# Adding the second Toeplitz combination to Q inside its PSUM bank, with ScalarE as the reader, in a fused conv-attention-STU kernel

## The chip, the cores and the metric

The kernel runs on one core of a Trainium2 chip. The metric is the device time of one execution in microseconds (us), median of three runs. Fractions of a microsecond are given in us unless marked ns. The engines are named PE (TensorE, matrix multiply; PEld is its weight load), DVE (VectorE), ACT (ScalarE), POOL (GpSimd) and SP (the engine that issues the transfers here). SBUF is the on-chip working memory, PSUM the small memory of eight banks that PE writes its results to.

## The reference, cut to what matters

Four batch items of 48 x 48 tokens with 128 channels go through two layers. Layer 0 is a gated selective scan over four directions. Layer 1 is full attention over the 2304 tokens of an item, followed by a spectral filter layer (STU), to which the change belongs:

```python
U_plus, U_minus = _stu_conv(phi, u, PADDED_SL)      # causal convolution of u with 16 filters
s = sigma ** SIGMA_POW
out = jnp.einsum('btkd,k,kde->bte', U_plus, s, Mpp)
out = out + jnp.einsum('btkd,k,kde->bte', U_minus, s, Mpm)
...
out = out + jnp.einsum('btd,de->bte', ui, Mu[i])    # autoregressive part, 3 taps
...
outs over frac in (1, 2, 4, 8): the same on x[:, :T // frac] with other M; summed with weights
```

The kernel does the causal convolutions as products with Toeplitz matrices on PE. It splits tokens by their index modulo 4, so that a convolution over 2304 tokens becomes short ones over 576, and uses the three-product form of a two-by-two convolution: one product with the sum of two inputs (Q), and two others that are each added to Q.

## The kernel before, in words

**Stages.** For each batch item b, `scans(b, ...)` runs layer 0's selective scan; then an epilogue and `attention` follow. PE has little to do in the scans, so other work is laid between their steps by `more(share)`, which draws pieces from a generator until a share of the columns is done. In `scans(0)` that work is `mixture` (weights of the STU); in `scans(1)` to `scans(3)` it is the STU of the item before, `stu_alone(b - 1, ps)`. The STU of the last item runs by itself at the end. So there are three mixed stages and one end stage with an STU.

**A scan unit** (`scan`, lines 453 to 459) is four steps: ACT makes `dA` with an Exp into one of two PSUM banks (`psa`), and DVE scans it (L458). `enter` (L450) and `times_c` (L467) are DVE or POOL products over 1536 columns; `spread` (L442) and `sum_c` (L475) are PE matmuls.

**An STU** goes over `items`: five blocks of rows of `BLOCKS` (0-128, 128-256, 256-384, 384-512, 512-576), 16 filters k each, 80 items. They are called blocks 0 to 4 below. An item makes six convolutions `conv(n, c, g)`: combination c = 0, 1, 2 and group g = 0, 1, in the order (0,0) (0,1) (1,0) (1,1) (2,0) (2,1). Each is a chain of matmuls over row blocks J (L969) into a PSUM tile of the pool `psc`, which has three banks with one tag, used in turn (four in the end stage). What reads the bank is `taken`: for c = 0, ACT copies it into the SBUF tile Q (L983); for c = 1 and 2, DVE writes the sum of the bank and Q into U (L994). This reader is kept in `late` and put into its engine's queue by `do_late`, at the end of the following convolution. `project` (L1031) multiplies the U of the item before with the weights G; it stands after (1,0), the third convolution. At the first item of a block, `end` transposes the last block's result through another `psc` tile, and `ended` (DVE) reads that.

**The Toeplitz tiles.** The moving operands are tiles `tt` (pool of four buffers), loaded by SP from DRAM `fd` (L942), each row overlapping. A tile holds `SLOT` = 1154 columns: all three c in block 0, c = 0 and 1 together and then c = 2 in block 1, one c each in blocks 2 to 4. `fetch(n, c)` is called after each convolution. It looks up the tile that holds c (`held`) and issues loads up to the third tile beyond it. A load waits until PE has read the last of the tile whose buffer it takes, four tiles earlier; it stands in SP's queue with the scans' loads `rep` and `bc`, in order.

All queues are in program order as written out by these generators.

Of the kernel before, what the change touches and what calls it, by code (L numbers as in the profile page):

```python
# [8 lines left out]
F32 = mybir.dt.float32  # L9
# [6 lines left out]
P = 128  # L16
# [38 lines left out]
def hybrid_kernel(ctx: ExitStack, tc: tile.TileContext, a: dict, out: bass.AP):  # L55
# [3 lines left out]
    nc = tc.nc  # L59
# [742 lines left out]
    def mixture(pool, ps):  # L802

        late = []

        def keep_(G, p, j, k, q):
            nc.scalar.copy(G[:, :, j], p)
            if j == 0:  # L810
                nc.sync.dma_start(gd[k, :, q], G.rearrange("p s j c -> p (s j) c"))

        for k in range(KF):
            M = [pool.two.tile([P, NF, C], F32, tag=f"M{j}", name=f"M{j}_{k}") for j in range(2)]
            for t, src in zip(M, ("M_phi_plus", "M_phi_minus")):
                nc.sync.dma_start(t, a[src][:, k].rearrange("i d e -> d i e"))

            W = pool.two.tile([P, 2, NF, P], F32, tag="W", name=f"W{k}")
            for i in range(NF):
                nc.scalar.activation(W[:, 0, i], ident, AF.Copy, scale=ws[:, k, i:i + 1])  # L820
                nc.scalar.activation(W[:, 1, i], nident, AF.Copy, scale=ws[:, k, i:i + 1])
            yield 0
            for q in range(2):
                G = pool.two.tile([P, 3, 2, C], F32, tag="Gm", name=f"Gm{k}_{q}")
                for j in (1, 0):
                    p = ps.psc.tile([P, 3, C], F32, tag="c", name=f"G{k}_{q}_{j}")
                    for i in range(NF):

                        n = NF - 1 - i if j else 1
                        if i == (NF - 1 if j else 0):  # L830
                            continue
                        for t in range(2):
                            nc.tensor.matmul(p[:, :n] if j else p[:, NF - 1 - i], W[:, q if t else 0, i],
                                             M[t][:, i].unsqueeze(1).to_broadcast([P, n, C]) if j else M[t][:, i],
                                             start=(t == 0 and (i == 0 or not j)),
                                             stop=(t == 1 and (i == NF - 2 or not j)))
                            yield n * C
                    if late:
                        keep_(*late.pop())
                    late.append((G, p, j, k, q))  # L840
        keep_(*late.pop())
# [58 lines left out]
    def stu(b, pool, ps):  # L900
# [10 lines left out]

        u, sums = us[b]
        items = [(blk, k) for blk in BLOCKS for k in range(KF)]
        tts, Gs, Q, U, now, nxt = {}, {}, {}, {}, {}, [0]
        late = []

        def do_late(n=0):
            while len(late) > n:  # L920
# [7 lines left out]

        order = [(n, cs) for n in range(len(items)) for cs in slots(n)]

        def fetch(n, c):


            held = next(i for i, (j, cs) in enumerate(order) if j == n and c in cs)
            while nxt[0] < min(held + 4, len(order)):
                i, cs = order[nxt[0]]
                (lo, hi, place, extra), k = items[i]
                w = hi + 1
                t = pool.four.tile([P, SLOT], F32, tag="tt", name=f"tt{b}_{i}_{cs[0]}")
                t = t[:, :2 * len(cs) * w].rearrange("p (e i) -> p e i", i=w)  # L940
                row = fd[k, cs[0], 0]
                nc.sync.dma_start(t, bass.AP(row.tensor, row.offset + LF - hi,  # L942
                                             [[1, P], [LF + P, 2 * len(cs)], [1, w]]))
                for x in cs:
                    tts[i, x] = t[:, 2 * (x - cs[0]):2 * (x - cs[0]) + 2]
                nxt[0] += 1

        def fetch_G(n):
            if n < len(items):
                (lo, hi, place, extra), k = items[n]  # L950
                m = 2 if extra else 1
                Gs[n] = pool.two.tile([P, 2, 2, C], F32, tag="G", name=f"G{b}_{n}")
                nc.sync.dma_start(Gs[n][:, :, :m], gd[k, :, :, place:place + m])

        def conv(n, c, g):

            (lo, hi, place, extra), k = items[n]
            w = hi - lo
            first = lo - (g == 1 and c != 1)
            nw = hi - first  # L960
            t = tts[n, c]
            p = ps.psc.tile([P, 512], F32, tag="c", name=f"cv{b}_{n}_{c}_{g}")
            p2 = p[:, :2 * nw].rearrange("p (e m) -> p e m", e=2)
            nb = (hi + P - 1) // P
            for J in range(nb):
                at = max(first, J * P) if J else first
                end = J * P - 1
                x = (sums[:, J, g], u[:, J, 2 + g], u[:, J, g])[c]
                nc.tensor.matmul(p2[:, :, at - first:], x, t[:, :, hi - 1 - at + J * P:end if end >= 0 else None:-1],  # L969
                                 start=(J == 0), stop=(J == nb - 1))  # L970
                if J < nb - 1:
                    yield 2 * (hi - at)
            do_late()
            late.append(lambda: taken(n, c, g, p, w, nw))
            yield 2 * (hi - at)

        def taken(n, c, g, p, w, nw):
            if c == 0:
                if g == 0:
                    U[n] = pool.two.tile([P, 8 * P], F32, tag="U", name=f"U{b}_{n}")[:, :8 * w].rearrange(  # L980
                        "p (i m) -> p i m", i=8)
                Q[g] = pool.two.tile([P, 2 * (P + 1)], F32, tag=f"Q{g}", name=f"Q{b}_{n}_{g}")[:, :2 * nw]
                nc.scalar.copy(Q[g], p[:, :2 * nw])  # L983
                return

            if g == 0:
                dst, src, q = U[n][:, c - 1::6], p[:, :2 * w], Q[g]
            elif c == 1:
                dst, src = U[n][:, 2:6:3], p[:, :2 * w]
                q = Q[g].rearrange("p (e m) -> p e m", e=2)[:, :, 1:]  # L990
            else:
                dst, src, q = U[n][:, 3:5], p[:, 1:1 + 2 * w], Q[g][:, 1:1 + 2 * w]
            src, q = [x if len(x.shape) == 3 else x.rearrange("p (e m) -> p e m", e=2) for x in (src, q)]
            nc.vector.tensor_tensor(dst, src, q, ALU.add)  # L994

        def begin(n):
# [28 lines left out]
        def project(n):  # L1025
            (lo, hi, place, extra), k = items[n]
            w = hi - lo
            p = now["p"].rearrange("p f r m -> p (f r) m")
            for q in range(2):
                for v, x in reversed(parts(w, extra)):  # L1030
                    nc.tensor.matmul(p[:, :, :v], Gs[n][:, q, x, :], U[n][:, 4 * q:4 * q + 4, :v], start=False,  # L1031
                                     stop=(k == KF - 1 and q == 1 and v == w))
                yield 4 * (w + extra)
            if k == KF - 1:
                late.append(lambda: kept(n, now["p"], w))
# [5 lines left out]
        def end(n):  # L1041
            (lo, hi, place, extra), k = items[n]
            w = hi - lo
            p = ps.psc.tile([P, 4, C], F32, tag="c", name=f"ot{b}_{n}")
            for f in range(2):
                for r in range(2):
                    i = 2 * f + r
                    nc.tensor.transpose(p[:w, 2 * r + f], now["o"][:, i * w:(i + 1) * w], ident)
            late.append(lambda: ended(n, p, lo, hi))
            yield 4 * w  # L1050
# [3 lines left out]
            nc.vector.tensor_tensor(t, t, p[:hi - lo], ALU.add)  # L1054
            nc.sync.dma_start(out[b, 4 * lo:4 * hi].rearrange("(p j) c -> p j c", j=4), t)

        fetch(0, 0)
        for n, (_, k) in enumerate(items):
            if k == 0:
                begin(n)  # L1060
            for c in range(3):
                for g in range(2):
                    yield from conv(n, c, g)
                    fetch(n, c)
                    if (c, g) == (0, 0):
                        fetch_G(n)
                    elif (c, g) == (1, 0) and n > 0:
                        yield from project(n - 1)
                    elif (c, g) == (2, 1) and k == 0:
                        if n > 0:  # L1070
                            yield from end(n - 1)
                        yield from ar(n)
        do_late()
        yield from project(len(items) - 1)
        do_late()
# [44 lines left out]
    start_y(0)  # L1120
    for b in range(B):
        sp = Stage(tc, f"h{b}", "left", s=(6, SB))
        ps = Stage(tc, f"b{b}", "right", psa=(2, PSUM), psy=(1, PSUM), psB=(1, PSUM), psc=(3, PSUM), psp=(1, PSUM))
        bank["mm"] = ps.psB, "B"
        if b == 0:
            mixed = Stage(tc, "m", "right", two=(2, SB))
# [42 lines left out]
        assert first or not more  # L1169
        ps.close()  # L1170
        back.close()
    ps = Stage(tc, "end", "right", psc=(4, PSUM), psp=(1, PSUM))
    for _ in stu_alone(B - 1, ps):
        pass
    ps.close()
# [54 lines left out]
```

## Time and profile before

| | |
|---|---|
| median of 3 runs | 6416.79 us (6412.86 to 6426.66) |
| the profiled execution, and its span | 6422.87 us, 6421.2 us |
| PE busy | 5440.6 us (85%) |
| DVE busy | 4823.6 us (75%) |
| POOL busy | 3842.7 us (60%) |
| ACT busy | 2800.0 us (44%) |
| DMA queue of SP (q1) | 1025.00 MB, 62.3% of 16 engines' span |
| first mixed stage (STU of item 0 beside the scans of item 1) | 1474 to 2597 us |
| end stage (STU of item 3 alone) | 5715 to 6421 us |

Busy shares over the whole span mix stages with different limits, so the prediction reads them by stage. A line of the page's list of groups gives line, engine, operation, tiles written and read, shapes and count; then busy time in us, mean duration in ns, and idle time of the engine just before, with what ended most of it. "A <- B" in a list of waits means that A's engine stood idle until B.

### The profile page before, as it was taken

To read this page: it belongs to the slowest core of one execution; us is meant where nothing else is said; L and a number is where in the kernel's file an instruction comes from. 1 tells how busy PE (TensorE), PEld (TensorE's weight loads), DVE (VectorE), ACT (ScalarE), POOL (GpSimd) and SP (SyncE) were. 2 spreads that over 40 slices of the span, in tenths; PEclk is the share of its full clock that TensorE was granted. 3 is DMA by queue.
4 is the path that set the end of the run, shared out by engine and by line. 5 is a ranking of instruction groups with operands and counts; after the bars stand their busy time and mean duration, and the time that the engine had idled before them with its cause. 6 is when DMAs were issued, how large, how long until landed. Compare 5 with 4: busy or idle time off the path is not lost.

```text
span 6421.2 us, 75575 instructions
## 1 busy us (share of the span) xinstructions
PE 5440.6 (85%) x25032; PEld 3353.1 (52%) x25032; DVE 4823.6 (75%) x6193; ACT 2800.0 (44%) x5053; POOL 3842.7 (60%) x1825
## 2 busy tenths in 40 slices
PE   3656555697999998888999999788999999789999
PEld 1222222444556566544556567544555567547789
DVE  6999999548999998558999998458999999322111
ACT  2555555244555554244555554244555554221000
POOL 1989888406778887306788887207788888100000
PEclk6787777799999999899999999899999999899999
DMA  4556566126878889127878889127788888025546
GB/s 104 139 138 151 139 144 148 40 55 162 199 196 215 216 221 247 59 62 165 198 195 217 222 218 256 39 64 179 189 203 215 219 224 246 28 67 151 154 141 212
DMA packets 658246, 1033.52 MB, mean 161 GB/s; under 512 B 93856, under 2 KB 515872, under 8 KB 633120
## 3 DMA queue, kind: packets, MB, share of 16 engines
q1 hardware_dynamic: 652032, 1025.00, 62.3%
q10 hardware_dynamic: 5824, 3.69, 0.3%
q8 instruction: 200, 3.28, 0.2%
q14 instruction: 190, 1.56, 0.1%
HBM read 905.79 MB, written 122.56 MB: 160 GB/s over the span
## 4 chain that ended last, share of the span: by engine, by line
PE 45%; DVE 24%; DMA 16%; POOL 4%; issue 4%; ACT 4%; SPq 3%; DVEq 0%; ACTq 0%; POOLq 0%
PE cv L969 19%; DVE s L458 11%; PE pr L1031 6%; DVE s L450 5%; DMA tt<-fd 5%; DMA rep<-dtdud 4%; PE s L714 4%; PE y L475 3%; PE o L707 3%; DMA bc<-xdd 3%; POOL s L467 3%; PE op L650 2%; PE B L442 2%; DVE xc L264 2%; DVE re L408 2%
## 5 line engine op out<-in xcount | busy, mean ns | idle before, releaser
L467 POOL TENSOR_TENSOR s<-s,bc 128x1536 f32<-128x1536 f32 x768 | 2647.8, 3449 | 179.8 <-DVE s L458 88.9
L458 DVE TENSOR_TENSOR_SCAN s<-dA,carry,s 128x384 f32<-128x384 f32 x2560 | 2458.1, 1000 | 190.1 <-ACT dA L455 189.0
L455 ACT ACTIVATE dA<-rep,A 128x384 f32<-128x384 f32 x3072 | 1782.0, 585 | 1627.0 <-DVE s L458 1622.2
L969 PE MATMUL cv<-tt,u 128*128 128x256 f32 (+3 forms) x7680 | 1632.6, 351 | 64.3 <-DVE U L994 38.0
L969 PEld LDWEIGHTS cv<-tt,u 128*128 128x128 f32 x7680 | 1259.7, 190 | 583.1 <-issue 266.1
L450 POOL TENSOR_TENSOR s<-rep,bc 128x1536 f32<-128x1536 f32 x288 | 994.2, 3452 | 95.3 <-DMA bc<-xdd 95.3
L969 PE MATMUL cv<-tt,us 128*128 128x256 f32 (+3 forms) x3840 | 841.0, 358 | 106.6 <-DVE U L994 55.3
L994 DVE TENSOR_TENSOR U<-cv,Q 128x256 f32<-128x256 f32 (+1 forms) x1280 | 480.3, 381 | 596.0 <-PE cv L969 581.2
L450 DVE TENSOR_TENSOR s<-rep,B 128x1536 f32<-128x1536 f32 x480 | 832.2, 1734 | 56.1 <-PE B L442 32.8
L475 PE MATMUL y<-s,csum 128*32 128x384 f32 x6144 | 720.6, 544 | 142.4 <-DVE ya L481 85.0
L969 PEld LDWEIGHTS cv<-tt,us 128*128 128x128 f32 x3840 | 639.7, 195 | 323.8 <-DVE U L994 89.7
L1031 PE MATMUL pr<-U,G 128*128 128x512 f32 (+4 forms) x2048 | 694.7, 469 | 3.5 <-DVE U L994 3.2
L983 ACT COPY Q<-cv 128x256 f32<-128x256 f32 (+3 forms) x640 | 224.0, 351 | 1027.2 <-PE cv L969 1025.5
L442 PE MATMUL B<-xd,spread 128*128 128x384 f32 x960 | 443.0, 546 | 177.4 <-DVE s L450 166.8
L458 DVE TENSOR_TENSOR_SCAN s<-dA,s 128x384 f32<-128x384 f32 x512 | 459.3, 938 | 70.9 <-ACT dA L455 70.7
L466 POOL COPY carry<-s 128x4 f32<-128x4 f32 x640 | 121.6, 190 | 574.8 <-DVE s L458 534.5
L1031 PEld LDWEIGHTS pr<-U,G 128*128 128x128 f32 x2048 | 334.5, 190 | 198.2 <-issue 137.0
L714 PE MATMUL s<-xnT 128*128 128x512 f32 (+1 forms) x720 | 357.9, 582 | 42.7 <-ACT xnT L676 23.4
L475 PEld LDWEIGHTS y<-s,csum 128*32 128x32 f32 x6144 | 127.7, 112 | 497.4 <-issue 336.3
L158 POOL TENSOR_TENSOR ln_vu<-ln_vu,mhalf 128x4 f32<-128x4 f32 (+1 forms) x20 | 26.8, 1341 | 602.0 <-DVE ln_vu L157 602.0
L716 ACT ACTIVATE e<-s,shift 128x512 f32<-128x512 f32 (+1 forms) x360 | 231.2, 644 | 314.1 <-PE s L714 313.6
L707 PE MATMUL o<-e,xn 128*128 128x512 f32 (+1 forms) x720 | 343.4, 560 | 4.5 <-ACT e L716 4.5
(157 smaller groups left out, 3638.1 us busy)
## 6 DMA issues: line engine op xcount, KB each, us to landing
rep<-dtdud SPq DMA_DIRECT2D x768, 384.0 KB, 7.8
tt<-fd SPq DMA_DIRECT2D x192, 577.0 KB, 5.5
bc<-xdd SPq DMA_DIRECT2D x2304, 48.0 KB, 3.4
tt<-fd SPq DMA_DIRECT2D x192, 513.0 KB, 4.5
tt<-fd SPq DMA_DIRECT2D x192, 385.0 KB, 4.3
dtdud<-re SPq DMA_DIRECT2D x768, 96.0 KB, 2.3
G<-gd SPq DMA_DIRECT2D x192, 256.0 KB, 5.3
tt<-fd SPq DMA_DIRECT2D x64, 514.0 KB, 5.6
```

Source lines behind the costliest of these rows:

```text
L442: nc.tensor.matmul(self.bt[:, :CS], spread[:, self.ch.k // 2, self.q].rearrange("p c j -> p (c j)"), self.ch.xd, start=True, stop=True)
L450: eng.tensor_tensor(s, self.ch.rep[self.h][:, 1], bt.unsqueeze(1).to_broadcast([P, G4, CS]), ALU.mult)
L455: nc.scalar.activation(dA[:, :CS], ch.rep[self.h][:, 0, g], AF.Exp, scale=A[:, ch.k, self.h * G4 + g, self.q:self.q + 1])
L458: nc.vector.tensor_tensor_scan(s, dA[:, CS - 1::-1] if ch.rev else dA[:, :CS], s, 0.0 if ch.first else carry[:, self.h, self.q, g:g + 1], ...
L467: nc.gpsimd.tensor_tensor(self.s, self.s, ch.bc[Q4 + self.q].unsqueeze(1).to_broadcast([P, G4, CS]), ALU.mult)
L475: nc.tensor.matmul(ch.y[g * DL:(g + 1) * DL, :CS], csum, self.s[:, g], start=(self.q == 0), stop=(self.q == Q4 - 1))
L707: nc.tensor.matmul(po[J][:, :w], xn[:, i], e[:, :w], start=(i == 0), stop=(i == NT - 1))
L714: nc.tensor.matmul(p[:, :w], xnT[:, i * P:(i + 1) * P], xnT[:, 512 * J:512 * J + w], start=True, stop=True)
L716: nc.scalar.activation(e[:, :w], p[:, :w], AF.Exp, bias=shift)
L969: nc.tensor.matmul(p2[:, :, at - first:], x, t[:, :, hi - 1 - at + J * P:end if end >= 0 else None:-1], start=(J == 0), stop=(J == nb - 1))
L994: nc.vector.tensor_tensor(dst, src, q, ALU.add)
L1031: nc.tensor.matmul(p[:, :, :v], Gs[n][:, q, x, :], U[n][:, 4 * q:4 * q + 4, :v], start=False, stop=(k == KF - 1 and q == 1 and v == w))
```

## The change

For c = 2 the matmuls no longer open a new accumulation in a bank of their own: they go on adding into the bank that still holds the c = 0 product of the same group (it has been copied to Q for c = 1). The sum is then already in PSUM, and ACT copies it into U; DVE's sum for c = 2 is gone. DVE still sums for c = 1. The three banks get tags of their own: `q0` and `q1` for the groups' c = 0 and 2, `c` for c = 1 (and for `end`'s transposes). The order of the six convolutions becomes (0,0) (1,0) (0,1) (2,0) (1,1) (2,1), and `fetch` takes the list of convolutions left in the item instead of c: a tile counts as held as long as one of these needs it. `project` of the item before stays after the third convolution, now (0,1). In the end stage each tag has two banks, six in all instead of four. `mixture` goes round the three tags.

```diff
@@ mixture
-                    p = ps.psc.tile([P, 3, C], F32, tag="c", name=f"G{k}_{q}_{j}")
+                    p = ps.psc.tile([P, 3, C], F32, tag=("c", "q0", "q1")[banks[0] % 3], name=f"G{k}_{q}_{j}")
+                    banks[0] += 1
@@ stu
+        banks = {}
+
+        convs = [(0, 0), (1, 0), (0, 1), (2, 0), (1, 1), (2, 1)]
...
-        def fetch(n, c):
-            held = next(i for i, (j, cs) in enumerate(order) if j == n and c in cs)
+        def fetch(n, left):
+            held = next(i for i, (j, cs) in enumerate(order) if j == n and any(c in cs for c, g in left))
...
-            p = ps.psc.tile([P, 512], F32, tag="c", name=f"cv{b}_{n}_{c}_{g}")
+            if c < 2:
+                p = banks[c, g] = ps.psc.tile([P, 512], F32, tag="c" if c else f"q{g}", name=f"cv{b}_{n}_{c}_{g}")
+            else:
+                p = banks[0, g]
...
-                                 start=(J == 0), stop=(J == nb - 1))
+                                 start=(c < 2 and J == 0), stop=(J == nb - 1), skip_group_check=(c == 2))
...
-                dst, src, q = U[n][:, 3:5], p[:, 1:1 + 2 * w], Q[g][:, 1:1 + 2 * w]
-            src, q = [x if len(x.shape) == 3 else x.rearrange("p (e m) -> p e m", e=2) for x in (src, q)]
+                dst, src = U[n][:, 3:5], p[:, 1:1 + 2 * w]
+            src = src.rearrange("p (e m) -> p e m", e=2)
+            if c == 2:
+                nc.scalar.copy(dst, src)
+                return
+            q = q if len(q.shape) == 3 else q.rearrange("p (e m) -> p e m", e=2)
             nc.vector.tensor_tensor(dst, src, q, ALU.add)
...
-            for c in range(3):
-                for g in range(2):
-                    yield from conv(n, c, g)
-                    fetch(n, c)
...
+            for i, (c, g) in enumerate(convs):
+                yield from conv(n, c, g)
+                fetch(n, convs[i:])
+                if i == 0:
+                    fetch_G(n)
+                elif i == 2 and n > 0:
+                    yield from project(n - 1)
+                elif i == 5 and k == 0:
+                    if n > 0:
+                        yield from end(n - 1)
+                    yield from ar(n)
@@ stages
-        ps = Stage(tc, f"b{b}", "right", psa=(2, PSUM), psy=(1, PSUM), psB=(1, PSUM), psc=(3, PSUM), psp=(1, PSUM))
+        ps = Stage(tc, f"b{b}", "right", psa=(2, PSUM), psy=(1, PSUM), psB=(1, PSUM), psc=(1, PSUM), psp=(1, PSUM))
-    ps = Stage(tc, "end", "right", psc=(4, PSUM), psp=(1, PSUM))
+    ps = Stage(tc, "end", "right", psc=(2, PSUM), psp=(1, PSUM))
```

More of the change, by code (lines that the diff above doesn't have):

```diff
@@ L806, in mixture @@
         late = []
+        banks = [0]
         def keep_(G, p, j, k, q):
@@ L1055, in ended @@
             nc.sync.dma_start(out[b, 4 * lo:4 * hi].rearrange("(p j) c -> p j c", j=4), t)
-        fetch(0, 0)
+        fetch(0, convs)
         for n, (_, k) in enumerate(items):
@@ L1060, in stu @@
                 begin(n)
-            for c in range(3):
-                for g in range(2):
-                    yield from conv(n, c, g)
-                    fetch(n, c)
[L1065 to L1072, printed above, removed]
+            for i, (c, g) in enumerate(convs):
[9 more added lines that the diff above has]
+                    yield from ar(n)
         do_late()
```

## The prediction

> **What bounds the kernel now.** I read the page's slices first, to see which stages the change touches.
>
> ```profile
> PE   3656555697999998888999999788999999789999
> ...
> DVE  6999999548999998558999998458999999322111
> ...
> DMA  4556566126878889127878889127788888025546
> ```
>
> Each digit is 160 us. The Toeplitz work (L969) lies in the three stretches where PE, DVE and DMA all stand at 8 or 9 (the mixed stages), and in the last five slices (the end stage), where DVE is nearly idle. The groups give the change's prices: sum, copy, and the scan that DVE is there for.
>
> ```profile
> L458 DVE TENSOR_TENSOR_SCAN s<-dA,carry,s 128x384 f32<-128x384 f32 x2560 | 2458.1, 1000 | 190.1 <-ACT dA L455 189.0
> ...
> L994 DVE TENSOR_TENSOR U<-cv,Q 128x256 f32<-128x256 f32 (+1 forms) x1280 | 480.3, 381 | 596.0 <-PE cv L969 581.2
> ...
> L983 ACT COPY Q<-cv 128x256 f32<-128x256 f32 (+3 forms) x640 | 224.0, 351 | 1027.2 <-PE cv L969 1025.5
> ```
>
> Then busy time in windows, cut at the blocks of the first mixed stage (block 0 to 4 downward; columns: window, length, busy PE, PEld, DVE, ACT, POOL with counts, clock, DMA share, GB/s).
>
> ```profile
> 1474.00:1630.00 156.00, 136.44 (x554) 72.51 (x554) 137.61 (x184) 78.81 (x148) 114.15 (x57) 0.97 0.76 179
> 1630.00:1839.00 209.00, 194.97 (x880) 113.35 (x880) 191.08 (x241) 107.36 (x195) 166.97 (x74) 0.96 0.78 190
> 1839.00:2094.00 255.00, 245.07 (x1179) 150.08 (x1178) 247.55 (x297) 140.18 (x246) 217.33 (x99) 0.99 0.88 217
> 2094.00:2392.00 298.00, 285.10 (x1371) 179.67 (x1370) 291.77 (x344) 161.59 (x282) 264.28 (x121) 0.99 0.85 219
> 2392.00:2597.00 205.00, 182.46 (x1339) 144.73 (x1339) 177.50 (x229) 93.12 (x175) 159.15 (x73) 0.95 0.87 232
> ```
>
> In blocks 2 and 3 DVE is 97-98% busy and PE 96%: two engines are at their limit together. In block 4 both drop to under 90% while the transfers are densest. The waits of that whole stage (1474 to 2597 us) say what stands between them:
>
> ```profile
> ACT Q L983 <- PE cv L969: 135.6, 92, 9.5
> ...
> DVE s L458 <- ACT dA L455: 69.2, 59, 5.3
> ...
> PE cv L969 <- DVE U L994: 31.4, 27, 3.9
> PE cv L969 <- DMA tt<-fd: 17.2, 5, 5.1
> ```
>
> Last, the timeline of PE, ACT and DVE at 2438 us, in block 4:
>
> ```profile
> 2437.98 2.91 PE L969 MATMUL cv<-tt,us 128*128 128x128 f32 x12 [5.13 <-DMA tt<-fd]
> ...
> 2440.49 0.27 ACT L983 COPY Q<-cv 128x128 f32<-128x128 f32 x1 [5.95 <-PE cv L969]
> ...
> 2441.28 1.02 DVE L458 TENSOR_TENSOR_SCAN s<-dA,carry,s 128x384 f32<-128x384 f32 x1 [5.34 <-ACT dA L455]
> ```
>
> A late tile stops PE for 5.13 us; ACT stands at the copy behind it for 5.95 us, with the next Exp in its queue, and DVE starves for 5.34 us. So in block 4 a late tile reaches the scans in full.
>
> **What the Trainium skill says.** "TensorE: Matmul & The Clock Gate", section on the architectural detail of the array, calls the ACT and DVE queues strict FIFO; the three lines above agree. "PSUM — Partial Sum Buffer", section "The four PSUM rules", allows a synchronised read of a partial sum in the middle of an accumulation group; the new c = 2 rests on that, and no run here shows it yet.
>
> **The change part by part.** Mixed stages count three times, the end stage once.
>
> *DVE sums removed.* Per stage 160 of 320 sums go: 128 of 256 columns (median 0.398 us) and 32 of 128 columns (0.267 us), so 50.9 + 8.5 = 59.5 us of DVE, 51 us of it in blocks 0 to 3. That is no path time: PE is idle only 56 us in these four blocks together (918 us less 861.6 busy), and with DVE eased PE is the limit. What I credit is PE's own wait for these sums: 31.4 us per stage, halved because half the banks are now read by ACT: 16 us, 48 us in all. Bounds: 0 and 51 us per stage. In block 4 and in the end stage DVE is no limit: nothing.
>
> *Copies added on ACT.* 160 per stage, taken as the Q copy's 0.351 us: 56 us, ACT from 581 to 637 us of 1123. In blocks 2 and 3 the scan is longer than the Exp (1000 against 585 ns), which hides a copy. In blocks 0 and 1 ACT already waits 83 us (1475 to 1950 us) for PE at its Q copies, and behind a waiting copy stands an Exp. The trace has no such copy for c = 2; bounds are 0 and another 69 us per stage (today's whole starvation). I take 4 us: 12 us in all.
>
> *PE.* The same matmuls; each bank is reused three convolutions after it was written, as before. The copy of Q must be done before (2,g) writes; two convolutions lie between, and PE waited for Q copies only 3.5 us per stage. Nothing.
>
> *`end`.* Its transposes now take bank `c`, whose sum (1,1) is queued on DVE one convolution before instead of two, and (1,0) of the next item then waits for `ended`. Four times per stage; the one such wait that shows is 3.1 us (ot <- U). Lower bound 0, upper 4 x 2 x 3 = 24 us; much of it lies under DVE's backlog: 3 us per stage, 9 us in all. The end stage has two such banks: nothing.
>
> *Toeplitz tiles.* This is the part that decides. With one c per tile (blocks 2 to 4), a tile was read by two neighbouring convolutions; now c = 0 spans positions 0-2, c = 1 positions 1-4, c = 2 positions 3-5. With four buffers, tile (n+1, c = 1) takes the buffer of (n, c = 0): from its last read to its first use lay six convolutions, and now lie four. The same for c = 2; c = 0 keeps six. Bytes, loads and SP's order are the same. I matched in the trace, for each load of the three stages, the last matmul on the old buffer, issue, landing and first use (medians, first mixed stage, us):
>
> | tile | lead before | release to issue | issue to landing | lead after |
> |---|---|---|---|---|
> | block 2, c=1 | 15.5 | 1.4 | 6.9 | 10.9 |
> | block 3, c=1 | 18.4 | 2.2 | 5.1 | 12.9 |
> | block 4, c=1 | 13.1 | 1.9 | 5.9 | 7.9 |
> | block 4, c=2 | 12.4 | 0.0 | 6.3 | 8.7 |
> | end stage, block 4, c=1 | 7.4 | 0.0 | 4.5 | 5.2 |
>
> Landing times spread (block 4 of the stage):
>
> ```profile
> DMA to landing us min/median/max: 3.6/6.3/12.6
> ```
>
> Shifting each load by the new release and use, c = 1 in block 4 is late in 9 or 10 of 16 items, by 26, 29 and 28 us in the three stages together; c = 2 by 6 to 9 us; blocks 2 and 3 together by 14, 9 and 22 us. The end stage misses by 0.1 us: nothing. These sums are no forecast yet: a stall at c = 1 gives c = 2 its time back, and fewer loads under way land sooner (4.5 us in the end stage). I take 15 of block 4's 28 us, and 5 of the 15 us of blocks 2 and 3, where DVE has a backlog under which PE may wait: 20 us per stage, 60 us in all. Bounds: 5 us per stage if landings fall to the end stage's, and about 50 us if all of it stays (152 us in three stages).
>
> **Sum:** -48 + 12 + 9 + 60 = +33 us. The profiled execution's own time is 6422.87 us (span 6421.2 and 1.7 around it) and would be 6456; it lies 6.1 us over the median, so against the median 6416.79 this is 6450 us.
>
> **The rivals.**
>
> *Likeliest, chance 0.43: shallower prefetch outweighs the relief,* 6430 to 6490.
>
> *Relief wins, 0.26, faster.* Place: blocks 0 to 3 of the mixed stages. If DVE is the true limit, 35 of its 51 us come back: -105 us, against 12 + 9 + a prefetch loss of 8 per stage (24): -60, so 6357 us. It decides from the point where relief per stage exceeds late tiles per stage plus 7 us. For it: DVE 97-98% busy for 553 us. Against: PE is at 96% in the same windows, and 59.5 us is the most that goes.
>
> *ACT becomes the gate, 0.19, slower still.* The tiles cost 30 us per stage, and ACT's doubled copies, each waiting for PE, starve the scans by 20 more: -48 + 90 + 60 + 9 = +111, so 6528 us. For it: the 2438 us chain. Against: in blocks 2 and 3 (1950 to 2420 us) ACT waits at Q copies only 11 us.
>
> *No difference, 0.12:* relief and late tiles cancel, or the reordering adds waits that hold the old pace.
>
> **How the numbers follow.** About 0.2% (13 us) is what a measurement can tell from no change. Slower 0.43 + 0.19 = 0.62, same 0.12, faster 0.26. Predicted 6450. The likeliest case alone spans 6430 to 6490. The range leaves out half of the faster case's lower tail and the upper tail of the ACT case: 6355 to 6530.
>
> **What would show it.** Right: 640 DVE sums instead of 1280, and 640 copies into U on ACT at 0.27 to 0.37 us; PE waiting for `tt` well over 17.2 us per mixed stage, mostly in block 4; block 4 longer than its 205 us by some 15 us; blocks 0 to 3 (918 us) shorter by about 10 us; the end stage within 2 us of its 706 us. Wrong: block 4 not longer (then landings have eased), blocks 0 to 3 shorter by over 25 us per stage (then DVE was the limit, not PE), or the scan's wait for Exp well over 69 us per stage outside block 4 (then ACT is the gate).

## The result, and the profile after

The changed kernel took 6405.99 us (median of 4 runs, 6404.10 to 6408.92) against 6414.82 us for the kernel before; ratio 0.9985, 95% interval 0.9968 to 1.0003. Measured again with 14 runs against 18: 6402.16 against 6413.73 us, **ratio 0.9981 (0.9973 to 0.9989)**. So the change makes the kernel 12 us faster, a little under the 0.2% that the prediction set as its bound, where 33 us slower was predicted.

The page of the changed kernel: the slices, and the groups that answer to those shown of before.

```profile
PE   3665565697999998888999998788999998889999
...
DVE  6999999548889998458899998458899998311000
...
DMA  4556566127888888127888888127888887025546
...
L458 DVE TENSOR_TENSOR_SCAN s<-dA,carry,s 128x384 f32<-128x384 f32 x2560 | 2442.5, 1000 | 246.3 <-ACT dA L455 244.1
...
L1007 DVE TENSOR_TENSOR U<-cv,Q 128x256 f32<-128x256 f32 (+1 forms) x640 | 244.4, 382 | 688.3 <-PE cv L978 679.9
...
L1004 ACT COPY U<-cv 128x256 f32<-128x256 f32 (+1 forms) x640 | 222.9, 348 | 676.1 <-PE cv L978 675.2
...
L992 ACT COPY Q<-cv 128x256 f32<-128x256 f32 (+3 forms) x640 | 223.0, 348 | 378.7 <-PE cv L978 375.2
```

The sums are halved and 640 copies into U stand on ACT, at 348 ns, as expected. DVE's busy time fell from 4823.6 to 4622.7 us, that is by 201 us, and the time by 12. The first mixed stage in windows, cut at its blocks (columns as in the prediction):

```profile
1471.00:1619.00 148.00, 131.83 (x554) 72.92 (x554) 125.28 (x151) 87.24 (x177) 110.99 (x56) 0.99 0.79 186
1619.00:1826.00 207.00, 193.59 (x881) 113.36 (x882) 185.28 (x213) 117.67 (x230) 167.75 (x74) 0.98 0.80 194
1826.00:2084.00 258.00, 246.27 (x1178) 151.69 (x1177) 236.71 (x264) 148.88 (x277) 219.48 (x100) 0.98 0.87 214
2084.00:2381.00 297.00, 286.74 (x1376) 181.07 (x1375) 281.67 (x314) 170.27 (x315) 264.60 (x122) 0.99 0.86 221
2381.00:2587.00 206.00, 183.29 (x1337) 144.97 (x1335) 170.89 (x195) 97.56 (x206) 158.47 (x72) 0.94 0.82 229
```

In blocks 2 and 3 DVE went from 97-98% to 92-95% busy; PE stands at 95-97% as before. The waits of that stage (1471 to 2587 us):

```profile
ACT U L1004 <- PE cv L978: 108.3, 86, 8.1
DVE s L458 <- ACT dA L455: 89.3, 78, 7.7
ACT Q L992 <- PE cv L978: 47.2, 34, 9.5
PE cv L978 <- DMA tt<-fd: 27.8, 15, 5.1
...
PE cv L978 <- DVE U L1007: 19.5, 17, 3.9
```

Beside before: PE waits 12 us less for DVE's sums (19.5 for 31.4), 11 us more for tiles (27.8 for 17.2), and the scan 20 us more for its Exp (89.3 for 69.2). A chain like the one at 2438 us before is still there, in block 4 at 2526 us (timelines of PE, ACT, DVE):

```profile
2526.40 4.14 PE L978 MATMUL cv<-tt,u 128*128 128x128 f32 x22 [5.07 <-DMA tt<-fd]
...
2528.91 0.27 ACT L1004 COPY U<-cv 128x128 f32<-128x128 f32 x1 [8.10 <-PE cv L978]
...
2529.69 1.93 DVE L458 TENSOR_TENSOR_SCAN s<-dA,carry,s 128x384 f32<-128x384 f32 x2 [7.68 <-ACT dA L455]
```

Now the copy for c = 2 is what holds the Exp back. The time by block, from the first Toeplitz matmul of a block to the first of the next one (block 4 and the end stage: to the last matmul), worked out from the traces, three mixed stages added up (us):

| kernel | block 0 | block 1 | block 2 | block 3 | block 4 | end stage |
|---|---|---|---|---|---|---|
| before | 468.6 | 632.8 | 763.2 | 895.9 | 599.3 | 699.0 |
| after | 442.3 | 617.7 | 769.9 | 888.2 | 622.7 | 700.7 |
| difference | -26.3 | -15.1 | +6.7 | -7.7 | +23.4 | +1.7 |

A gain in blocks 0, 1 and 3 and a loss in block 4 nearly cancel. PE's wait for tiles rose by 37 us in the three stages, half of it in block 4 and half in blocks 2 and 3, where it was nothing before.

### The profile page after: what moved, and what is told of

Read it like the earlier page. It is cut to its first block, busy times and chain, and to the rows that moved or that the text cites. A ratio compares the mean times of both kernels' runs of the same rounds, so it can differ in the third digit from the quotient of the medians.

```text
span 6402.6 us, 75570 instructions
## 1 busy us (share of the span) xinstructions
PE 5427.8 (85%) x25032; PEld 3364.4 (53%) x25032; DVE 4622.7 (72%) x5553; ACT 2980.6 (47%) x5693; POOL 3840.5 (60%) x1825
## 4 chain that ended last, share of the span: by engine, by line
PE 49%; DVE 20%; DMA 17%; POOL 4%; issue 4%; ACT 4%; SPq 3%; DVEq 0%; ACTq 0%; POOLq 0%
PE cv L978 22%; DVE s L458 8%; PE pr L1044 7%; DMA tt<-fd 6%; DMA rep<-dtdud 4%; PE y L475 4%; DVE s L450 4%; PE s L714 4%; DMA bc<-xdd 3%; PE o L707 3%; POOL s L467 3%; PE B L442 2%; PE op L650 2%; DVE xc L264 2%; DMA G<-gd 2%
## 5 line engine op out<-in xcount | busy, mean ns | idle before, releaser
L467 POOL TENSOR_TENSOR s<-s,bc 128x1536 f32<-128x1536 f32 x768 | 2646.4, 3447 | 177.3 <-DVE s L458 93.3
L978 PE MATMUL cv<-tt,u 128*128 128x256 f32 (+3 forms) x7680 | 1649.9, 354 | 131.2 <-DMA tt<-fd 68.1
L978 PE MATMUL cv<-tt,us 128*128 128x256 f32 (+3 forms) x3840 | 855.4, 352 | 35.2 <-DMA tt<-fd 26.0
L1007 DVE TENSOR_TENSOR U<-cv,Q 128x256 f32<-128x256 f32 (+1 forms) x640 | 244.4, 382 | 688.3 <-PE cv L978 679.9
L1004 ACT COPY U<-cv 128x256 f32<-128x256 f32 (+1 forms) x640 | 222.9, 348 | 676.1 <-PE cv L978 675.2
L714 PE MATMUL s<-xnT 128*128 128x512 f32 (+1 forms) x720 | 356.9, 581 | 44.7 <-ACT xnT L676 23.4
```

Source lines behind the costliest of these rows:

```text
L467: nc.gpsimd.tensor_tensor(self.s, self.s, ch.bc[Q4 + self.q].unsqueeze(1).to_broadcast([P, G4, CS]), ALU.mult)
L714: nc.tensor.matmul(p[:, :w], xnT[:, i * P:(i + 1) * P], xnT[:, 512 * J:512 * J + w], start=True, stop=True)
```

## The experiments

All times are medians; ratios are to the kernel before on the same chip, with 95% intervals. Three chips were used, with the kernel before at 6413.73 us (the first four kernels), 6415.01 us (`order5`, `after5`, `dve_twice`, `hyb03`) and 6413.90 us (`before5`, `hyb5`, `order5_p3`), so the chips differ by about 1 us. The interval of a single ratio is wider: about 8 us each way for most kernels here, 5 us for `after_2` and `before5`.

**The changed kernel again** (`after_2`).

> The changed kernel once more, for a tighter interval. Blocks 0 to 3 of the three mixed stages together were 42 us shorter in the first profile and block 4 of them 23 us longer, the end stage 2 us longer. If that balance holds, the ratio lies at 0.997 to 0.999 with an interval that now excludes 1; if the first result was chance, the ratio is within 0.0005 of 1.

6402.16 us, 0.9981 (0.9973 to 0.9989): the small gain is real.

**The new order alone** (`order_only`): PSUM and readers as before.

```diff
-            if c < 2:
-                p = banks[c, g] = ps.psc.tile([P, 512], F32, tag="c" if c else f"q{g}", name=f"cv{b}_{n}_{c}_{g}")
-            else:
-                p = banks[0, g]
+            p = ps.psc.tile([P, 512], F32, tag=("c", "q0", "q1")[banks[0] % 3], name=f"cv{b}_{n}_{c}_{g}")
+            banks[0] += 1
...
-            if c == 2:
-                nc.scalar.copy(dst, src)
-                return
```

> The kernel before with the new order of convolutions and the new fetch alone: c = 2 again has a bank of its own in the rotation of three, and VectorE sums it with Q. Theory 1 (two effects: VectorE's relief gives some 14 us per mixed stage, the shallower prefetch of Toeplitz tiles takes some 9): no relief, the prefetch loss stays, so 20 to 40 us slower than before, ratio 1.003 to 1.006, with PE waiting for tiles 22 to 29 us per mixed stage and block 4 longer by 3 to 12 us per stage. Rival 3 (the order itself is what brings the gain, by spreading the readers of the banks): 5 to 20 us faster than before, with blocks 0 and 1 shorter by about 10 us per stage.

6482.01 us, 1.0102 (1.0089 to 1.0116): 68 us slower than before, so the order is no source of the gain (rival 3 falls), and it costs far more than theory 1 said. PE's wait for tiles is 24 to 28 us per mixed stage, within the expectation; block 4 grew by 21 us over three stages, but blocks 0 to 2 by 6, 7 and 26 us, where PE's wait for tiles rose by under 5 us in all. What the change does beyond the order is worth 80 us (6402 against 6482).

**DVE instead of ACT reads the bank** (`dve_reader`): accumulation and order stay.

```diff
-                nc.scalar.copy(dst, src)
+                nc.vector.tensor_copy(dst, src)
```

> The changed kernel with VectorE instead of ScalarE copying the c = 2 sum out of its bank: the accumulation in PSUM and the order stay, the reader does not move. Theory 1: VectorE saves only the second operand, so its relief is nearly nothing while the prefetch loss stays: 25 to 45 us slower than the changed kernel, ratio to before 1.003 to 1.006. Rival 2: PE waits for VectorE at the banks as before (31 us instead of 19 us per mixed stage), 20 to 40 us slower than the changed kernel too; the two part at the kernel with VectorE's time put back. If ScalarE's copies are a burden on the scan's Exp (rival ACT), this kernel is as fast as the changed one or faster, and the scan waits for Exp less than before (52 to 57 us per stage outside block 4 would fall to 40 or less).

6465.87 us, 1.0082 (1.0069 to 1.0096): 64 us slower than the changed kernel, more than either theory said. Its group of copies on the page, and waits of its first mixed stage (1470 to 2602 us):

```profile
L1004 DVE COPY U<-cv 128x256 f32<-128x256 f32 (+1 forms) x640 | 244.8, 383 | 395.8 <-PE cv L978 394.1
...
DVE s L458 <- ACT dA L455: 47.9, 43, 4.5
PE cv L978 <- DVE U L1004: 27.2, 22, 3.9
PE cv L978 <- DVE U L1007: 11.5, 14, 1.7
```

At 383 ns the copy costs DVE what the sum did (381 ns): accumulating in PSUM saves none of DVE's time as long as DVE reads the bank. Of the 80 us, some 16 belong to the accumulation, for a reason that no run shows, and 64 to the move to ACT. PE's wait for DVE at the banks is 39 us (27.2 and 11.5), against 19.5 in the changed kernel; the second and third stage differ by as much, so the move takes about 60 us of these waits away (5 come back as waits for ACT's copies). The scan's wait for Exp is 48 us, against 89 in the changed kernel; `dve_twice` below says how much of that goes with ACT's copies.

**DVE's time put back, first try** (`dve_load`).

```diff
                 nc.scalar.copy(dst, src)
+                idle = pool.one.tile([P, 2 * (P + 1)], F32, tag="idle", name=f"idle{b}_{n}_{g}")
+                nc.vector.tensor_tensor(idle[:, :2 * w], Q[g][:, :2 * w], Q[g][:, :2 * w], ALU.add)
                 return
```

> The changed kernel with VectorE's time put back: beside each ScalarE copy of c = 2 VectorE adds Q to itself into an unused tile (two SBUF inputs, the same columns as the sum that went). Nothing waits for its result. Theory 1 (VectorE's time is what was relieved): the 42 us of blocks 0 to 3 are gone, so 30 to 50 us slower than the changed kernel, ratio to before 1.004 to 1.007. Rival 2 (VectorE's time is worth nothing, PE is the limit; the gain is that PE waits less for banks that ScalarE reads): as the changed kernel within 10 us, ratio 0.997 to 1.000.

6908.87 us, 1.0771 (1.0757 to 1.0786), ten times what any theory said. The added sum is no copy of the one removed:

```profile
L1006 DVE TENSOR_TENSOR idle<-Q 128x256 f32<-128x256 f32 (+1 forms) x640 | 810.6, 1267 | 0.0
```

It lasts 1267 ns on average instead of 381. The last section returns to this; the run doesn't decide between the theories.

**DVE's time put back, second try** (`dve_twice`): each c = 1 sum is made twice, with one operand in PSUM like the sums that went.

```diff
+            idle = pool.one.tile([P, 2 * P], F32, tag="idle", name=f"idle{b}_{n}_{g}")
+            nc.vector.tensor_tensor(idle[:, :2 * w].rearrange("p (e m) -> p e m", e=2), src, q, ALU.add)
             nc.vector.tensor_tensor(dst, src, q, ALU.add)
```

> The changed kernel with VectorE making each sum for c = 1 twice, first into a tile that nobody reads. Operands and length are those of the sums that the change took away (one from PSUM, one from SBUF), so VectorE's 60 us per mixed stage come back while PE's order, the accumulation and ScalarE's copies stay; bank c is held 0.4 us longer. Theory 1 (VectorE's time is what the change saves): 50 to 80 us slower than the changed kernel, 6450 to 6480 us, about what the new order costs with VectorE summing. Rival 2 (VectorE's time is covered; what counts is that ScalarE reaches the banks sooner): at most 25 us slower, under 6428 us.

6457.35 us, 1.0067 (1.0053 to 1.0080): 55 us slower than the changed kernel. The groups on the page, and waits of the first mixed stage (1473 to 2604 us):

```profile
L1009 DVE TENSOR_TENSOR U<-cv,Q 128x256 f32<-128x256 f32 (+1 forms) x640 | 247.8, 387 | 0.0
L1008 DVE TENSOR_TENSOR idle<-cv,Q 128x256 f32<-128x256 f32 (+1 forms) x640 | 244.1, 381 | 634.4 <-PE cv L978 605.5
...
DVE s L458 <- ACT dA L455: 66.8, 55, 7.2
PE cv L978 <- DVE U L1009: 30.0, 20, 4.6
```

The added sums have the right length, and DVE is busy for 1044 us of the first mixed stage, as before (1046; the changed kernel 1000). Three quarters of the added 244 us, some 180 us, lie in the mixed stages and cost 55. Rival 2 allowed 25 at most; with DVE's time put back, most of the 64 us are gone. What the run can't part: the added sum stands ahead of the one that frees bank c, which is so held about 0.38 us longer, and PE's wait for DVE's sums rose by 10 us per stage (30.0 for 19.5 in the first). How much of the 55 us is this longer hold is not shown; a run with the added work behind the sum was not made.

Here DVE's load is that of `dve_reader` while ACT makes the copies, so the two side by side show what ACT's copies do to the scans: the wait for Exp is 67 us against 48 in the first stage, and 19 to 25 us longer in each of the three. The rest of the way to the changed kernel's 89 us goes with a DVE that has less to do. The move to ACT pays in spite of the copies.

**A fifth tile buffer** (`order5`, `after5`, `before5`): each tile is fetched one further ahead.

```diff
-            while nxt[0] < min(held + 4, len(order)):
+            while nxt[0] < min(held + 5, len(order)):
...
-                t = pool.four.tile([P, SLOT], F32, tag="tt", name=f"tt{b}_{i}_{cs[0]}")
+                t = pool.five.tile([P, SLOT], F32, tag="tt", name=f"tt{b}_{i}_{cs[0]}")
...
-                Q[g] = pool.two.tile([P, 2 * (P + 1)], F32, tag=f"Q{g}", name=f"Q{b}_{n}_{g}")[:, :2 * nw]
+                Q[g] = (pool.two if g else pool.one).tile([P, 2 * (P + 1)], F32, tag=f"Q{g}", name=f"Q{b}_{n}_{g}")[:, :2 * nw]
...
+            if k == 4:
+                begin_res(n - 4)
```

> The kernel with the new order alone, and a fifth buffer for the Toeplitz tiles, each tile fetched one further ahead. The space comes from one Q tile of group 0 and one residual tile instead of two, the residual loaded at the fifth filter of a block. With five buffers every tile has at least seven convolutions from the last read of its buffer to its first use, more than the six of the kernel before. Theory 1a (the order's cost of 68 us is the shallower prefetch): most of it goes, 6400 to 6430 us, ratio 0.998 to 1.003. Rival 1b (only the 8 us per mixed stage go by which PE waited longer for tiles; the rest of the cost comes from how the new order spaces VectorE's sums): 6445 to 6465 us, ratio 1.005 to 1.008.

> The changed kernel with the fifth buffer, by the same edits. Theory 1a (prefetch costs the changed kernel what the order alone lost): 50 to 68 us faster than the changed kernel, 6335 to 6355 us, ratio 0.988 to 0.991. Rival 1b (the waits for tiles alone, 7 to 11 us per mixed stage over the kernel before, most of them in block 4): 20 to 40 us faster, 6362 to 6382 us, ratio 0.992 to 0.995, with block 4 at 195 to 200 us instead of 206 to 209.

> The kernel before (old order, VectorE summing) with the fifth tile buffer, by the same edits. It waits for tiles only 17 us per mixed stage, 11 to 13 of them in block 4. If the fifth buffer's worth is the tile waits that it removes, 0 to 20 us faster than before, 6395 to 6415 us; then the 34 us that it gave the changed kernel belong to that kernel's longer holding of tiles. If deeper prefetch helps every kernel alike, 28 to 34 us faster, 6381 to 6387 us.

`order5` took 6454.16 us, 1.0063 (1.0050 to 1.0075), 28 us under the order with four buffers. `after5` took 6367.86 us, 0.9925 (0.9911 to 0.9938), 34 us under the changed kernel. `before5` took 6422.05 us, 1.0011 (1.0004 to 1.0018): 8 us slower than before, where neither theory had it. PE's wait for tiles in the first mixed stage of `after5` (1472 to 2580 us):

```profile
PE cv L978 <- DMA tt<-fd: 17.2, 5, 4.6
```

That is the figure of the kernel before; in the other two stages it is 14.5 and 15.2 us (before: 14.6 and 16.2). In `before5` these waits didn't fall at all (49 us in three stages, 48 before), so the kernel before had nothing of this to win. The late tiles that come with the change cost some 30 us, as rival 1b had it. It may be up to 8 us more: the same edits leave one buffer fewer for Q and for the residual, and block 0, where one tile serves all three c, is 3 to 7 us longer (three stages) in each of the kernels with five buffers than in its counterpart with four. Bytes are the same in all of them; what counts is how long before its use a transfer may start. Counted on the edit, c = 2 gets six convolutions with five buffers, not seven as expected; that is still what the kernel before had. Block 4 of the three stages went from 206, 208 and 208 us (changed kernel) to 206, 195 and 197 us (`after5`).

The order keeps a cost of 39 us with five buffers, 32 beside `before5`. The waits of blocks 0 to 3 of its first mixed stage (1473 to 2401 us):

```profile
PE cv L976 <- DVE U L1002: 38.6, 34, 3.9
DVE U L1002 <- PE cv L976: 13.4, 15, 2.0
PE cv L976 <- DVE res L1065: 4.9, 2, 2.6
PE cv L976 <- DMA tt<-fd: 4.4, 1, 4.4
```

In the same blocks before: 30.2, 3.0, none and 4.0 us; in `before5`: 34.4, 3.0, none and 4.1 us. Tiles are no longer late; PE waits 13 us more than before for DVE's readers of the banks, 9 more than in `before5`, and DVE 10 us more for PE, with the same sums merely asked for in another order.

**The projection moved** (`order5_p3`): `elif i == 3 and n > 0:` in place of 2.

> The kernel with the new order alone and five tile buffers, still 39 us over the kernel before; here the projection of the item before stands after the fourth convolution instead of the third. If that cost comes from where the projection falls between VectorE's sums (in the old order it stood right after the first convolution that VectorE reads, and gave VectorE time), 20 to 40 us of it go: 6415 to 6435 us. If it comes from the spacing of VectorE's sums themselves, the time stays at 6445 to 6463 us.

6471.54 us, 1.0089 (1.0076 to 1.0103), 17 us slower than `order5`, which neither case had: one place later the projection costs more. One place earlier, right after the first convolution that DVE reads, as in the old order, was not run, so its place isn't ruled out as a part of the 39 us. That the rest is the spacing of DVE's sums is what the waits suggest; no run shows it.

**The old scheme in block 4** (`hyb03`, and `hyb5` with five buffers): below the test is that of the changed scheme; where it fails, order, banks and sums are as before.

```diff
+        def kept_bank(n):
+            return n < 4 * KF
+
+        def convs_of(n):
+            if kept_bank(n):
+                return [(0, 0), (1, 0), (0, 1), (2, 0), (1, 1), (2, 1)]
+            return [(c, g) for c in range(3) for g in range(2)]
```

> The changed scheme (order, accumulation in the bank, ScalarE as reader) in blocks 0 to 3 only; block 4 runs as in the kernel before, its tiles held by two neighbouring convolutions and VectorE summing. Both theories on the tiles: block 4 returns to 195 to 205 us per mixed stage from 206 to 209 and the rest stays as in the changed kernel, so 10 to 30 us faster than it, 6372 to 6392 us, ratio 0.993 to 0.997. If VectorE's relief is what matters in block 4 as well, nothing is gained: 6395 to 6415 us.

> The changed scheme in blocks 0 to 3, the old one in block 4, and five tile buffers. If the old scheme in block 4 and the fifth buffer cure the same loss (late tiles in block 4), they don't add: 6355 to 6368 us, as with either alone or up to 10 us less. If they are two losses they add: 6330 to 6345 us.

`hyb03` took 6370.19 us, 0.9931 (0.9918 to 0.9943), 32 us under the changed kernel and 2 us under its range, with block 4 at 196 to 204 us per stage. `hyb5` took 6357.73 us, **0.9909 (0.9896 to 0.9923)**, the fastest of all, 56 us under the kernel before. Over `after5` it gains only 10 us: the two cure mostly the same loss.

## Why the prediction was wrong

**What held.** *Engines at the limit together:* most of the 201 us that DVE lost were not path time, and PE stayed at its 95-97% in blocks 2 and 3. *Toeplitz tiles:* the mechanism (c = 1 and 2 with four convolutions of lead instead of six, late most of all in block 4, stalls passed on through ACT's copy to the scan) is what the traces show and the fifth buffer cures. Block 4 was to grow by 15 us per stage; it grew by 8. *PE and the end stage:* 1.7 us of change against nothing predicted. *Copies:* 348 ns against 351 taken. (The 83 us of waiting that it read for blocks 0 and 1 take in 111 us of block 2; blocks 0 and 1 alone have 74.)

**The terms that failed**, as the sum had them (us):

| term | predicted | measured |
|---|---|---|
| DVE sums removed, with the copies on ACT and the accumulation | -48 + 12 = -36 | -80 (`after_2` less `order_only`) |
| Toeplitz tiles | +60 | +28 (`order_only` less `order5`), +34 (`after_2` less `after5`); up to 8 more each if the edits' own cost in `before5` is added |
| `end` and anything else in the order | +9 | +39 (`order5` less before), 32 (less `before5`) |
| sum | +33 | about -12 |

1. *Toeplitz tiles* was too large: 60 us against 28 to 42. The shifted loads gave 152 us of lateness, and 60 were kept. Matching the loads of the changed kernel in the same way shows where the size was lost, in block 4 at c = 1: the lead is 9.0 to 9.6 us (medians of the three stages) where 7.9 was forecast, and the loads are issued at once (0.0 us after release) where the 1.9 us of before had been kept; landing takes 5.3 to 6.0 us, about as before. So 5 of 16 tiles in each stage land too late or just in time, not 9 or 10.

2. *DVE sums removed* credited 16 us per stage, half of the 31.4 us that PE waited for these sums in the old order. In the new order PE waits longer for them, 39 us per stage as long as DVE reads every c = 1 and c = 2 bank (`dve_reader`), and moving the reader takes 20 of these away, about 60 us in all, beside the 64 by which the time falls. The other 16 of the 80 us, the accumulation, had been priced at nothing; what ACT's copies cost is inside the 64 and wasn't measured apart. The upper bound of 51 us per stage held.

3. *The order itself* had been priced only through the tiles and `end`. Some 30 of its first 39 us were missing: "each bank is reused three convolutions after it was written, as before" was true of the distance, but "Nothing" didn't follow from it. Which engine reads the bank at which place also changed, and `order5` shows PE waiting more at DVE's readers. In the changed kernel ACT reads four of six banks and this wait falls to 19.5 us, so moving the reader is what makes the new order affordable. Why the old spacing was cheaper stays open.

Steps 2 and 3 are two sides of one wait, PE's for DVE at the banks: the order lengthens it, the move to ACT shortens it. They err by 44 and 30 us in opposite directions, and their net is 14 us off (26 if the buffers' own cost is taken out of the order); the tiles are off by 18 to 32. So the sign was not lost in one term: with either of the two errors put right the forecast would have lain between 1 and 19 us slower, and only with both of them is it a gain. That it came out only 45 us from the measured time, with the relief at half its size and the order almost free, is luck.

The relief rival (6357 us) named the place of the gain, but with 105 us for 80 and no cost for the order. The ACT rival's 20 us of longer waiting for Exp are there (89.3 against 69.2 us), but the time didn't follow. Nearest was the rival that had the least chance but named both effects: relief and late tiles cancel, and the reordering adds waits.

## What to carry to other kernels

Where two engines are both above 95% busy, time taken from one is worth a share of itself: here about 0.3 us for each microsecond of sums put back (`dve_twice`, the longer hold of a bank included). The idle time that the profile puts down to an instruction is that of the present order of work: here the new order raised PE's wait for DVE at the banks from 31 to 39 us per mixed stage, and moving the reader brought it to 19. So a reordering should be priced apart from what it enables. This one cost 68 us, some 30 of them because tiles were held over more convolutions of their item, and one more buffer, or the old order in the one block with short convolutions, or both, turned a gain of 12 us into 45 to 56. Moving the reader of a PSUM bank to an idler engine gave 64 of the 80 us, and making the read simpler on the same engine saved none of its time.

## What the runs showed of the hardware

A DVE sum of two SBUF tiles beside a busy POOL is far longer than alone. `dve_load`'s added sum, by tile, in the first mixed stage (1472 to 2740 us) and in the end stage (6200 to 6890 us):

```profile
L1006 DVE TENSOR_TENSOR idle<-Q x158: 315/1460/3604, 1477.3 to 2739.6; 128x256 f32<-128x256 f32 x128, 128x128 f32<-128x128 f32 x30
...
L1006 DVE TENSOR_TENSOR idle<-Q x155: 279/414/424, 6211.0 to 6885.9; 128x256 f32<-128x256 f32 x126, 128x128 f32<-128x128 f32 x29
```

Minimum, median and maximum in ns: alone the median is 414, beside the scans 1460, and the longest, 3604, is about one POOL product (3447 ns on the page of the changed kernel). One of them on the timeline:

```profile
1913.39 3.44 POOL L450 TENSOR_TENSOR s<-rep,bc 128x1536 f32<-128x1536 f32 x1
...
1914.07 3.05 DVE L1006 TENSOR_TENSOR idle<-Q 128x256 f32<-128x256 f32 x1
```

It begins inside a POOL product and ends 0.29 us after it. All 352 added sums of the mixed stages that last over 500 ns end so, 0.15 to 0.29 us after a POOL instruction does. The Trainium skill agrees, in "SBUF — State Buffer", section "Who interferes with whom": a VectorE instruction with two SBUF inputs contends with a GpSimd instruction that reads SBUF, through ports that work as an exclusive lock, where the order of issue decides who waits. The profile counts that time as DVE busy, with no idle time before it, so it appears as no wait. The sums of the kernel before, with one operand in PSUM, take 398 ns at the median in the first mixed stage and 424 in the end stage, so POOL doesn't lengthen them.

Second, for these sizes a DVE copy from PSUM (383 ns) is no shorter than a DVE sum of PSUM and SBUF (381 ns), and ACT's copy takes 348 ns.
